# A hand-made order for VectorE, ScalarE and TensorE in the second part of a sparse graph-attention kernel

## The chip, the cores and the metric

The kernel runs on one core of a Trainium2 chip. The metric is the device time of one execution in microseconds. The kernel before took 1316.58 us (median of 9 runs, 1310.54 to 1321.33).

A core has five engines, each with its own queue of instructions that it takes in order: TensorE (PE; matrix multiplies, PEld is its loading of weights), VectorE (DVE), ScalarE (ACT), GpSimd (POOL) and SyncE (SP). An instruction that needs another engine's result waits on a semaphore, and what stands behind it on its engine waits with it. DMAs are issued from POOL and SP.

## The reference

3327 nodes with 1024 features in float32, and a symmetric 0/1 matrix `adj` of 3327 x 3327 with ones on the diagonal and few others:

```python
h = jnp.maximum(_layernorm(x, axis=-1), 0.0)
f = h @ Wf + bf
g = h @ Wg + bg
e = jax.nn.relu(f @ g.T)
scores = jnp.where(adj > 0, e, NEG)
attention = jax.nn.softmax(scores, axis=1)
x = x + attention @ (h @ W + bW)
```

Only the pairs that `adj` connects count. Some nodes have 37 neighbours, most 11 to 25.

## The kernel before, in words

The kernel works on the edges alone (`edge_path`; the dense path behind it runs only if a check finds a node with too many neighbours).

**First part (to about 250 us).** It reads `adj`, makes of each row a list of neighbours, normalises x into h (kept in HBM as `hd`), folds Wf and Wg into one matrix `A_sb` so that a node's score with a neighbour is a dot of q = h A (plus a bias) with the neighbour's h, and sorts the nodes by their number of neighbours. The change leaves this part alone.

**Second part.** The sorted nodes are taken in 26 tiles of 128. `CAPS` holds how many neighbours a tile can have; `ORDER` is the order of processing, and the text counts tiles in that order, 0 to 25. Tile 2 has 37 neighbours, tile 3 has 25, and so on down to 17 in tile 16, 13 in tiles 23 and 24 and 11 in tile 25. Tiles of more than 16 neighbours (2 to 16) are worked in two chunks: the first has 10 (19 in tile 2), the second the rest. The others have one chunk. A chunk is a *unit* of the main loop.

For each tile:

- GpSimd gathers the rows h of neighbour k, one per node, into one of 26 buffers G (`dot`, gather L983 through the helper at L356), and later gathers the tile's own x onto the result (`result`, L1097) and scatters the result out (`finish`, L1102). `fetch` (L894) brings the list and the own rows of a tile two tiles ahead.
- VectorE makes the *dots*: a row of G times q, added up, one score each (L986, followed by a short read of the accumulator). A dot reads all 1025 columns of q.
- `softmax`: VectorE takes relu and mask (L995) and the negated *maximum* of the chunk (L997; L999 joins it with the earlier chunk's). ScalarE makes the exponentials (L1002). For a second chunk it makes the factor `al` (L1005) and scales the running sum y by it (L1011); for a first chunk it scales row 0 by its weight, which becomes y (L1050). `l` and `rs` (L1006, L1009) are the total and its inverse.
- `combine`: the rows are added up with their weights. 11 per tile in tiles 3 to 23 (20 in tile 2, 5 to 7 in the others) are *sums* on VectorE (L1052), y += weight x G. The others, only in the tile's last chunk, are scaled on ScalarE (L1046) and added on TensorE, by transposing them into one PSUM accumulator (`sum_transposed`, L1026). `on_tensor` says how many.
- `project`: TensorE adds y itself to that accumulator, ScalarE copies it out (L1060), TensorE multiplies it with W (32 matmul records, L1068, 13.9 us), ScalarE scales the result (L1090).
- Meanwhile the q of the tile two ahead is made: `turned` transposes its own rows (L917), `taken` copies them (L924), `third` multiplies them with one third of `A_sb` (L936), `emptied` copies that third of q out on ScalarE (L946) and puts the bias into the freed PSUM bank (`filled`, L884). The last third stands after y's transposes in `project`, and its copy after the softmax of the next unit.
- `failed` (L1113), called once in tile 23, brings the check's flag together: a small matmul (L1120) and a cast on VectorE (L1121).

**What sets the order.** A planner orders the instructions of each engine in this part, by priority (roughly the program's order) and by what it reckons to be ready. `in_line` (L864) ties the marked instructions of TensorE and ScalarE into one chain in program order; the others, and all of VectorE and GpSimd, the planner places. With `AHEAD = 3`, the first three dots of the next unit are written behind a unit's softmax, the other dots of that unit at its beginning. In the program that results, VectorE alternates a tile's sums with dots of the next unit; behind the last maximum of a two-chunk tile comes a sum first, behind a first-chunk maximum come two to seven dots, and behind the maximum of a one-chunk tile one to three sums.

Of the kernel before, what the change touches and what calls it, by code (L numbers as in the profile page):

```python
# [33 lines left out]
AHEAD = 3  # L34
# [262 lines left out]
def edge_path(ctx: ExitStack, tc: tile.TileContext, x, adj, Wf, bf, Wg, bg, W, bW, out, flag):  # L297
# [563 lines left out]
    queue = {}  # L861

    @contextmanager
    def in_line():  # L864
        with ExitStack() as both:
            for ins in queue.values():
                both.enter_context(tc.issue_after(ins.ins))
            yield


# [15 lines left out]

    one = small.tile([P, 1], FP, name="one")
    tc.keep_in_program_order(nc.scalar.activation(one, ident[:, :1], AF.Exp))

    for at in range(2):  # L890
        filled(p_q, "ps_q", vb, QB, 6 + at, True)
        filled(p_o, "ps_o", bWb, CB, at, True)
# [15 lines left out]
    def turned(s):  # L908
        e = st[s]
        e["hT"] = hTpool.tile([P, KD, P], FP, name="hT")  # L910
        e["ps_t"] = []
        for g in range(0, KD, 4):
            ps = p_t.tile([P, 4, P], FP, name="ps_t")
            e["ps_t"].append(ps)
            with in_line():
                for k in range(4):
                    ins = nc.tensor.transpose(ps[:, k, :], e["hp"][:, (g + k) * P : (g + k + 1) * P], ident)  # L917
            queue["pe"] = ins

    def taken(s):  # L920
        e = st[s]
        for g, ps in enumerate(e["ps_t"]):
            with in_line():
                queue["act"] = nc.scalar.copy(e["hT"][:, 4 * g : 4 * g + 4, :], ps)  # L924

    def third(s, i):
# [7 lines left out]
        with in_line():  # L934
            for k in range(KD):
                ins = nc.tensor.matmul(  # L936
                    ps[:, :QB], e["hT"][:, k, :], A_sb[:, k, o : o + QB], start=False, stop=(k == KD - 1),
                    skip_group_check=True,
                )
        queue["pe"] = ins  # L940

    def emptied(s, i):
        e = st[s]
        at = 3 * ORDER.index(s) + i
        with in_line():
            ins = nc.scalar.copy(e["q"][:, i * QB : (i + 1) * QB], e["ps_q"][i][:, :QB])  # L946
            if at + 2 < 3 * NT:
                ins = filled(p_q, "ps_q", vb, QB, at + 2)
        queue["act"] = ins
# [29 lines left out]
    def dot(s, k, behind=None):  # L979
# [5 lines left out]
        with tc.issue_after(behind.ins) if behind else ExitStack():  # L985
            nc.vector.tensor_tensor_reduce(  # L986
                junk, g, e["q"][:, :D], 1.0, e["q"][:, D : D + 1], op0=ALU.mult, op1=ALU.add,
                accum_out=e["sc"][:, k : k + 1],
            )

    def softmax(s, k0, k1, last):
# [5 lines left out]
        nc.vector.tensor_reduce(nm, sc, AX.X, ALU.max, negate=True)  # L997
        if k0:
            nc.vector.tensor_tensor(nm, nm, e["nm"], op=ALU.min)  # L999
        l = small.tile([P, 1], FP, name="l")  # L1000
        with in_line():
            nc.scalar.activation(sc, sc, AF.Exp, bias=nm, accum_out=l)  # L1002
        if k0:
            al = small.tile([P, 1], FP, name="al")
            nc.scalar.activation(al, e["nm"], AF.Exp, bias=nm, scale=-1.0)  # L1005
            nc.vector.scalar_tensor_tensor(l, e["l"], al, l, op0=ALU.mult, op1=ALU.add)  # L1006
        if last:
            e["rs"] = small.tile([P, 1], FP, name="rs")
            nc.vector.reciprocal(e["rs"], l)  # L1009
        if k0:  # L1010
            queue["act"] = nc.scalar.activation(e["y"], e["y"], AF.Copy, scale=al)  # L1011
        e["nm"], e["l"] = nm, l
# [19 lines left out]
    def combine(s, k0, k1, last, ahead=None):  # L1032
        e = st[s]
        if not k0:
            e["y"] = G[s, 0]
# [3 lines left out]
        for k in range(k0, k1):  # L1039
            p = e["sc"][:, k : k + 1]  # L1040
            g = G[s, k]
            if k in pe:
                if k == pe[-1] and ahead is not None:
                    taken(ahead)
                with in_line() if k == pe[-1] else ExitStack():
                    queue["act"] = nc.scalar.activation(g, g, AF.Copy, scale=p)  # L1046
                queue["pe"] = sum_transposed(e, g, e["first"], False)
                e["first"] = False
            elif k == 0:
                queue["act"] = nc.scalar.activation(y, y, AF.Copy, scale=p)  # L1050
            else:
                e["summed"] = nc.vector.scalar_tensor_tensor(y, g, p, y, op0=ALU.mult, op1=ALU.add)  # L1052

    def project(s, then=None):
        e = st[s]
        yT = yTpool.tile([P, KD, P], FP, name="yT")
        with in_line():
            queue["pe"] = sum_transposed(e, e["y"], e["first"], True)
            for g in range(0, KD, 4):
                queue["act"] = nc.scalar.copy(yT[:, g : g + 4, :], e["yT"][:, g : g + 4, :])  # L1060
# [3 lines left out]
        for o in range(OH):  # L1064
            ps = banks.pop(("ps_o", OH * ORDER.index(s) + o))
            with in_line():
                for k in range(KD):
                    ins = nc.tensor.matmul(  # L1068
                        ps, yT[:, k, :], W_sb[:, k, o * CB : (o + 1) * CB], start=False, stop=(k == KD - 1),
                        skip_group_check=True,  # L1070
                    )
            e["o"].append(ps)
            queue["pe"] = ins
# [3 lines left out]
    def result(s):  # L1077
# [3 lines left out]
        for o in range(OH):  # L1081
# [7 lines left out]
            with in_line():  # L1089
                ins = nc.scalar.activation(to, ps, AF.Copy, scale=e["rs"])  # L1090
                if at < OH * NT:
                    ins = filled(p_o, "ps_o", bWb, CB, at, scale=st[ORDER[at // OH]]["l"])
            queue["act"] = ins
# [143 lines left out]
```

## Time and profile before

| | |
|---|---|
| median of 9 runs | 1316.58 us (1310.54 to 1321.33) |
| profiled execution, its own time | 1324.93 us |
| its span, first to last instruction | 1323.1 us |
| VectorE busy | 1157.7 us (87%) |
| TensorE busy | 1125.1 us (85%) |
| GpSimd, ScalarE busy | 892.6, 609.8 us |
| dots L986 | 468 of 1284 ns, 601.0 us |
| sums L1052 | 275 of 1286 ns, 353.5 us |
| mean granted TensorE clock | 0.941 |

The profile is of one execution. A line of a timeline gives the start, the duration, the engine, the line of the kernel, the operation, what it writes and reads, and in brackets how long its engine stood idle before it and what ended that. A line of waits gives the engine and operation that waited, what released it, the sum of the waits, their number and the longest. Durations of neighbours overlap a little, so the pace of an engine is read from start to start. Busy times of TensorE are modelled ends.

### The profile page before, as it was taken

What the parts mean: (1) busy time and instruction counts of PE and PEld (TensorE: products, weight loads), DVE (VectorE), ACT (ScalarE), POOL (GpSimd) and SP (SyncE); (2) the same over time, 40 slices, a digit from 0 to 9 for tenths busy, and PEclk for the clock granted to TensorE, in tenths of its full rate; (3) what the DMA queues carried; (4) which work ended last, traced back from release to release, by engine and by line L of the source; (5) the groups of instructions that cost most, each with busy time, mean ns of one, the idle gap of its engine ahead of it and who ended that gap; (6) DMA issues with size and microseconds to landing.
All of it is one profiled execution on the core that took longest, in us unless ns stands there. A gap on an engine that the chain in (4) does not pass through costs nothing.

```text
span 1323.1 us, 14316 instructions
## 1 busy us (share of the span) xinstructions
PE 1125.1 (85%) x4488; PEld 708.9 (54%) x4488; DVE 1157.7 (87%) x2205; ACT 609.8 (46%) x943; POOL 892.6 (67%) x678
## 2 busy tenths in 40 slices
PE   2799962967855999898899898999999899999995
PEld 2566631643525575566555555555655566555553
DVE  6899977575899889899999999999999999999980
ACT  5899976133306255345442554433344433333350
POOL 8999973384675777776766667676666666666611
PEclk9899985976977989999999999999999999999998
DMA  9999995786786998898888888888888688888821
GB/s 372 416 390 405 410 320 190 259 284 241 232 296 240 300 301 286 292 316 293 287 292 287 293 295 289 284 267 291 290 289 278 215 283 289 275 288 285 270 80 50
DMA packets 101802, 374.44 MB, mean 283 GB/s; under 512 B 14747, under 2 KB 18490, under 8 KB 98519
## 3 DMA queue, kind: packets, MB, share of 16 engines
q0 software_dynamic: 80624, 290.96, 66.1%
q1 hardware_dynamic: 21094, 82.49, 16.2%
q8 instruction: 37, 0.61, 0.2%
q14 instruction: 47, 0.39, 0.1%
HBM read 344.11 MB, written 29.30 MB: 282 GB/s over the span
## 4 chain that ended last, share of the span: by engine, by line
issue 30%; DVE 27%; PE 14%; DMA 12%; POOL 9%; ACT 7%; SPq 0%; POOLq 0%; another core or an unknown queue 0%; DVEq 0%; ACTq 0%
DVE G L1052 11%; POOL G L356 8%; DMA G<-hd,pi 5%; DVE junk L986 5%; DVE cand L482 5%; PE ps_o L1068 4%; PE yT_ps L1026 4%; PE ps_A L552 4%; ACT G L1046 3%; PE ps_q L936 2%; DMA r<-in_adj_dram 2%; DMA res<-in_x_dram,perm 1%; DVE sc L986 1%; DMA xt<-in_x_dram 1%; ACT G L1011 1%
## 5 line engine op out<-in xcount | busy, mean ns | idle before, releaser
L356 POOL DMA_INDIRECT G<-hd,pi x454 | 541.5, 1193 | 205.3 <-issue 100.6
L986 DVE CUSTOM_DVE_ANT_0 junk<-G,q 128x1024 bf16<-128x1024 f32 x468 | 601.0, 1284 | 39.5 <-DMA G<-hd,pi 18.1
L1052 DVE SCALAR_TENSOR_TENSOR G<-G,sc 128x1024 f32<-128x1024 f32 x275 | 353.5, 1286 | 39.9 <-ACT G L1011 22.6
L1068 PE MATMUL ps_o<-W_sb,yT 128*128 128x512 f32 x832 | 363.3, 594 | 6.3 <-ACT yT L1060 6.3
L936 PE MATMUL ps_q<-A_sb,hT 128*128 128x342 f32 x1152 | 347.7, 456 | 9.7 <-issue 9.4
L1026 PE MATMUL yT_ps<-ident,G 128*128 128x128 f32 x1544 | 211.0, 289 | 87.9 <-ACT G L1046 62.4
L936 PEld LDWEIGHTS ps_q<-A_sb,hT 128*128 128x128 f32 x1152 | 216.9, 192 | 119.8 <-issue 17.9
L1068 PEld LDWEIGHTS ps_o<-W_sb,yT 128*128 128x128 f32 x832 | 157.4, 189 | 200.6 <-issue 188.1
L1026 PEld LDWEIGHTS yT_ps<-ident,G 128*128 128x128 f32 x1544 | 182.0, 149 | 119.8 <-ACT G L1046 76.3
L419 POOL TENSOR_TENSOR r<-r,iotaj 128x1664 f32<-128x1664 f32 (+3 forms) x50 | 183.8, 3739 | 12.1 <-ACT r L412 12.1
L1046 ACT ACTIVATE G<-G,sc 128x1024 f32<-128x1024 f32 x167 | 182.4, 1142 | 0.0
L1002 ACT ACTIVATE sc<-sc,nm 128x10 f32<-128x10 f32 (+11 forms) x41 | 12.5, 304 | 343.3 <-DVE nm L999 251.7
L552 PE MATMUL ps_A<-WgT,WfT 128*128 128x342 f32 x432 | 131.5, 463 | 2.3 <-ACT WfT L547 2.3
L482 DVE MAX8 cand<-r 128x8 f32<-128x208 f32 (+2 forms) x416 | 119.1, 360 | 4.2 <-POOL r L419 3.3
L946 ACT COPY q<-ps_q 128x342 f32<-128x342 f32 x72 | 31.4, 437 | 166.4 <-PE ps_q L936 129.6
L552 PEld LDWEIGHTS ps_A<-WgT,WfT 128*128 128x128 f32 x432 | 82.2, 194 | 43.2 <-issue 3.0
L412 ACT ACTIVATE r<-r 128x3327 f32<-128x3327 int32 (+3 forms) x27 | 77.3, 2862 | 7.8 <-DMA r<-in_adj_dram 7.8
L356 POOL DMA_INDIRECT res<-in_x_dram,perm x25 | 43.2, 1727 | 51.3 <-ACT res L1090 43.4
L1102 POOL DMA_INDIRECT out_dram<-res,perm x25 | 30.7, 1226 | 69.2 <-DMA res<-in_x_dram,perm 67.7
L924 ACT COPY hT<-ps_t 128x512 f32<-128x512 f32 x48 | 25.4, 581 | 75.5 <-PE ps_t L917 75.5
L356 POOL DMA_INDIRECT pi<-pd,perm x26 | 29.6, 1139 | 34.6 <-DMA cd<-cand 17.9
L536 PE MATMUL ps_tr<-ident,A_sb 128*128 128x128 f32 x128 | 23.1, 343 | 26.5 <-DMA A_sb<-in_L_gnn_Wg_dram 23.3
(139 smaller groups left out, 718.7 us busy)
## 6 DMA issues: line engine op xcount, KB each, us to landing
r<-in_adj_dram SPq DMA_DIRECT2D x24, 1663.5 KB, 12.2
xt<-in_x_dram SPq DMA_DIRECT2D x25, 512.0 KB, 13.0
hd<-xt SPq DMA_DIRECT2D x25, 512.0 KB, 10.5
G<-hd,pi POOLq DMA_INDIRECT x454
A_sb<-in_L_gnn_Wg_dram SPq DMA_DIRECT2D x8, 512.0 KB, 17.3
A_sb<-in_L_gnn_Wf_dram SPq DMA_DIRECT2D x8, 512.0 KB, 11.8
W_sb<-in_L_gnn_W_dram POOLq DMA_DIRECT2D x1, 4096.0 KB
cd<-cand SPq DMA_DIRECT2D x25, 64.0 KB, 12.2
```

Source lines behind the costliest of these rows:

```text
L356: return nc.gpsimd.indirect_dma_start(out=to, out_offset=None, in_=table, in_offset=bass.IndirectOffsetOnAxis(ap=idx, axis=0), **kw,)
L412: nc.scalar.activation(r[:n, b:e], a[:n, b:e], AF.Sign, accum_out=to)
L419: eng.tensor_mul(r[:n, b:e], r[:n, b:e], iotaj[:n, b:e])
L482: nc.vector.max(cands[t][:n, s * 8 : s * 8 + 8], r[:n, s * SW : min(N, (s + 1) * SW)])
L552: nc.tensor.matmul(ps[:, :QB], WfTs[c][:, k, :], WgT[:, k, o : o + QB], start=(k == 0), stop=(k == KD - 1))
L936: ins = nc.tensor.matmul(ps[:, :QB], e["hT"][:, k, :], A_sb[:, k, o : o + QB], start=False, stop=(k == KD - 1), skip_group_check=True,)
L946: ins = nc.scalar.copy(e["q"][:, i * QB : (i + 1) * QB], e["ps_q"][i][:, :QB])
L986: nc.vector.tensor_tensor_reduce(junk, g, e["q"][:, :D], 1.0, e["q"][:, D : D + 1], op0=ALU.mult, op1=ALU.add, accum_out=e["sc"][:, k : k ...
L1026: ins = nc.tensor.matmul(e["yT"][:, c, :], g[:, c * P : (c + 1) * P], ident, is_transpose=True, start=(first and c % 4 == 0), stop=(last a ...
L1046: queue["act"] = nc.scalar.activation(g, g, AF.Copy, scale=p)
L1052: e["summed"] = nc.vector.scalar_tensor_tensor(y, g, p, y, op0=ALU.mult, op1=ALU.add)
L1068: ins = nc.tensor.matmul(ps, yT[:, k, :], W_sb[:, k, o * CB : (o + 1) * CB], start=False, stop=(k == KD - 1), skip_group_check=True,)
```

## The change

All instructions of the second part on VectorE, ScalarE and TensorE are put under `manual_schedule`: these three engines take them in the order in which the program writes them. The chain `in_line` and the tie of the last tile's dots to earlier sums go. GpSimd and SP stay with the planner.

The program's order is rewritten for it. `AHEAD` is 2: from the third unit on, two dots of the next unit are written behind each maximum, after the copy of q's last third. `combine` then takes a function `between`, which writes one more dot of the next unit after each sum. What is left of the unit's dots comes at its beginning. `softmax` writes `al`, the exponential and the scaling of y next to each other, and the totals move into a new function `totalled` behind the two dots. The matmul and cast of `failed` stay in their place in the program, behind the rest of tile 23 and ahead of tile 24; the loads of the flag move to the end.

```diff
-AHEAD = 3
+AHEAD = 2
...
-    def dot(s, k, behind=None):
+    def dot(s, k):
...
-    def softmax(s, k0, k1, last):
+    def softmax(s, k0, k1):
...
         nc.vector.tensor_reduce(nm, sc, AX.X, ALU.max, negate=True)
+        l = small.tile([P, 1], FP, name="l")
         if k0:
             nc.vector.tensor_tensor(nm, nm, e["nm"], op=ALU.min)
-        l = small.tile([P, 1], FP, name="l")
-        with in_line():
-            nc.scalar.activation(sc, sc, AF.Exp, bias=nm, accum_out=l)
+            e["al"] = small.tile([P, 1], FP, name="al")
+            nc.scalar.activation(e["al"], e["nm"], AF.Exp, bias=nm, scale=-1.0)
+        nc.scalar.activation(sc, sc, AF.Exp, bias=nm, accum_out=l)
         if k0:
-            al = small.tile([P, 1], FP, name="al")
-            nc.scalar.activation(al, e["nm"], AF.Exp, bias=nm, scale=-1.0)
-            nc.vector.scalar_tensor_tensor(l, e["l"], al, l, op0=ALU.mult, op1=ALU.add)
+            nc.scalar.activation(e["y"], e["y"], AF.Copy, scale=e["al"])
+        else:
+            e["y"] = G[s, 0]
+            nc.scalar.activation(e["y"], e["y"], AF.Copy, scale=e["sc"][:, :1])
+        e["nm"] = nm
+        e["ls"] = (e.get("l"), l)
+        e["l"] = l
+
+    def totalled(s, k0, last):
+        e = st[s]
+        if k0:
+            before, l = e["ls"]
+            nc.vector.scalar_tensor_tensor(l, before, e["al"], l, op0=ALU.mult, op1=ALU.add)
         if last:
             e["rs"] = small.tile([P, 1], FP, name="rs")
-            nc.vector.reciprocal(e["rs"], l)
-        if k0:
-            queue["act"] = nc.scalar.activation(e["y"], e["y"], AF.Copy, scale=al)
-        e["nm"], e["l"] = nm, l
+            nc.vector.reciprocal(e["rs"], e["l"])
...
             else:
-                e["summed"] = nc.vector.scalar_tensor_tensor(y, g, p, y, op0=ALU.mult, op1=ALU.add)
+                nc.vector.scalar_tensor_tensor(y, g, p, y, op0=ALU.mult, op1=ALU.add)
+                between()
...
+    with tc.manual_schedule(engines={
+        mybir.EngineType.Activation, mybir.EngineType.DVE, mybir.EngineType.PE
+    }):
...
+            dots(s, range(k0, k1))
...
+            softmax(s, k0, k1)
+            if late:
+                emptied(late.pop(), 2)
+            covered = AHEAD if i > 1 else 0
+            dots(s2, range(a, min(b, a + covered)))
+            totalled(s, k0, last)
...
+            coming = iter(range(a + covered, b) if i > 1 and s != ORDER[-2] else ())
+
+            def between(s2=s2, coming=coming):
+                for k in coming:
+                    dots(s2, [k])
+                    break
+
+            combine(s, k0, k1, last, ahead, between)
...
+                if not at or i + 1 == len(units) or units[i + 1][2] == CAPS[units[i + 1][0]]:
+                    rest()
+                    rest = None
+                if at + 2 == NT - 1:
+                    failed()
+        finish(done_with.pop())
+        bad = nc.values_load(flag[0:1, 0:1], min_val=0, max_val=1 << 20)
+        result(ORDER[-1])
+        finish(ORDER[-1])
```

In the resulting program VectorE has, for a two-chunk tile, "maximum, two dots, totals, sum, dot, sum, seven dots" and then, in the next tile's first chunk, "maximum, two dots, and nine times sum, dot". For a one-chunk tile it has "maximum, two dots, rs, eleven times sum, dot, and the dots that are left". Tiles 0 and 1 have their sums in a row and then their successor's dots.

## The prediction

> **What bounds the kernel now.** I read the page's busy times first, then the waits of VectorE in the second part, then the three engines in order of time around one maximum, and last the end of the execution.
>
> ```profile
> span 1323.1 us, 14316 instructions
> PE 1125.1 (85%) x4488; PEld 708.9 (54%) x4488; DVE 1157.7 (87%) x2205; ACT 609.8 (46%) x943; POOL 892.6 (67%) x678
> ```
>
> VectorE and TensorE are both nearly full. The second part runs from about 277 us; it holds 468 dots (L986) and 275 sums (L1052). On VectorE a dot or sum starts 1.20 us after its predecessor where the two kinds alternate, 1.33 us where a dot follows a dot. So 743 of them cost at least 892 us of about 1030. What VectorE still waits for in that part:
>
> ```profile
> DVE G L1052 <- ACT G L1011: 22.6, 15, 1.7
> DVE res L1084 <- PE ps_o L1068: 20.0, 2, 13.9
> DVE G L1052 <- ACT G L1050: 14.4, 10, 4.1
> DVE junk L986 <- ACT q L946: 14.1, 2, 13.8
> DVE l L1006 <- ACT al L1005: 6.5, 10, 0.7
> DVE rs L1009 <- ACT sc L1002: 2.9, 8, 0.5
> ```
>
> The first, third and last two lines are the waits after a maximum: 46.4 us in all, the most that covering them could win. The other two are one early wait and the end. Around one maximum (VectorE, then ScalarE):
>
> ```profile
> 727.64 0.15 DVE L999 TENSOR_TENSOR nm<-nm 128x1 f32<-128x1 f32 x1
> 728.44 0.22 DVE L1006 SCALAR_TENSOR_TENSOR l<-l,al 128x1 f32<-128x1 f32 x1 [0.65 <-ACT al L1005]
> 730.52 1.28 DVE L1052 SCALAR_TENSOR_TENSOR G<-G,sc 128x1024 f32<-128x1024 f32 x1 [1.66 <-ACT G L1011]
> ```
> ```profile
> 727.83 0.30 ACT L1002 ACTIVATE sc<-sc,nm 128x10 f32<-128x10 f32 x1 [18.23 <-DVE nm L999]
> 728.13 0.28 ACT L1005 ACTIVATE al<-nm 128x1 f32<-128x1 f32 x1
> 729.35 1.14 ACT L1011 ACTIVATE G<-G,al 128x1024 f32<-128x1024 f32 x1
> 730.39 0.42 ACT L946 COPY q<-ps_q 128x342 f32<-128x342 f32 x1
> 745.23 0.45 ACT L946 COPY q<-ps_q 128x342 f32<-128x342 f32 x1 [3.15 <-PE ps_q L936]
> 747.58 0.30 ACT L1002 ACTIVATE sc<-sc,nm 128x10 f32<-128x10 f32 x1 [1.42 <-DVE nm L997]
> ```
>
> See two things. The copy at 730.39 is the last third of the next tile's q: it starts 2.6 us after the maximum. And the copy at 745.23, first third of a later q, holds ScalarE back until TensorE delivers: 17.4 us after the maximum at 727.8; the next exponential stands behind it. VectorE arrives 1.4 us later than that, so nothing is lost. The end:
>
> ```profile
> 1239.02 0.19 PE L1120 MATMUL ps_t<-onesf,bad 128*1 128x1 f32 x2 [0.24 <-ACT hT L924]
> 1245.18 0.14 DVE L1121 CAST flag<-ps_t 1x1 int32<-1x1 f32 x1
> ```
>
> The check's matmul runs ahead of tile 23's y transposes here, and its cast fits between sums.
>
> **The change, part by part.** Tiles are counted in processing order. TensorE's matmuls keep their order, except the check's. ScalarE gets, after each maximum: (al), exponential, y scaling, copy of the last third, bias fill, then the row scalings. VectorE gets a fixed order. GpSimd's gathers keep their order by tile. In tiles 20 to 24 the gather-add of an earlier result now stands behind 1 to 4 of a tile's row gathers (3 to 5 before), and the fetch of a later tile's own rows (L904) behind some ten of them. Of 26 buffers a tile of 15 leaves 10 to run ahead, so I cost this at 0 and keep it as a rival. The finishing scatter still follows two gathers later. SP issues nothing that moves.
>
> *A. Two dots behind the maximum of a tile's last chunk, tiles 6 to 16.* They are dots of the next tile. A dot reads the whole q, so it waits for the copy of the last third, which in the new order follows exponential, al and y scaling: starts 0.04 + 0.20 + 0.10 + 0.18 + 1.04, copy 0.42, is 2.0 us. Today VectorE waits 0.65 + 1.66 = 2.3 us here in the tiles up to 11 and 1.2 us in tiles 12 to 16. So the wait is renamed, not covered. Dots following dots go from about 11 to 8 a tile: -3 x 0.13 = -0.4. Six cycles at -0.7, four at +0.4, plus 0.4 twice from B: about -2. A full walk of the same cycles (38.1 against 36.3 to 37.1 for 17 rows, 40.5 against 41.0 for 19) gives +3. I take 0; bounds -4 and +4.
>
> *B. The sums of the next tile's first chunk, tiles 3 to 6.* From last-chunk maximum to next maximum VectorE now has 2.0 wait, two dots 2.5, l and rs 0.35, sum-dot-sum 3.6, seven dots 9.2, maximum 0.35: 18.0 us; then two dots, so the first sum is due at 20.6. It also needs the exponential and y scaling behind ScalarE's copy of the first third, 2.5 us after that copy starts. The copy starts 28.8, 28.0, 23.6 and 19.5 us after the maxima at 406.19, 459.05, 509.23 and 556.42 (435.00, 487.00, 532.85, 575.95), because these tiles scale 16 to 10 rows on ScalarE at 1.05 us each. So the sum waits until 31.3, 30.4, 26.1, 22.0. Before, the planner filled this time with up to seven dots behind the maximum; now two. What is left after it: 9 sums and (rows - 12) dots, 27.7, 25.1, 23.7, 22.4 us for 25, 23, 22, 21 rows. Cycles 59.0, 55.5, 49.8, 44.5 against 52.9, 50.2, 47.2, 43.5 measured: +6.1, +5.3, +2.6, +1.0 = +15. Bounds: +8 if TensorE's clock is full here (it was not: below), +20.
>
> *C. Tiles of one chunk, 17 to 23.* The two dots again need the next q's last third, now produced late: last sum, y transposes 0.95 + 0.05, last third's matmuls 4.65, copy 0.45 + 0.05. That is 6.1 us, then two dots 2.5, rs 0.2, ten pairs 24.0, the eleventh sum 1.2: a cycle of 34.1 us from last sum to last sum, even where VectorE's own work for 13 rows is 31. Before, two sums stood behind the maximum and the dots waited for nothing. From 997.17 (tile 16) to the end of tile 23's projection at 1269.90 it was 272.7 us. Now: first maximum 26.3, plus 2.0, to the last sum 28.0 (56.2); tiles 18, 19, 20 each 34.3 by VectorE's own work; 21 to 23 each 34.1; projection 19.5: 281. +8. Bounds 0 (TensorE's own cycle, 32.2 us at 1107 to 1139, holds instead) and +12.
>
> *D. The check.* Its matmul now stands behind tile 23's projection on TensorE, and its cast stands ahead of tile 24's maximum in VectorE's queue. So VectorE stops until that projection ends (last sum + 19.5). Queued behind: all of tile 24 and 25. From the end of the projection: cast and maximum 0.75, wait 2.0, two dots 2.6, rs 0.2, six sums 7.2, nine dots 12.0, maximum 0.35, exponential and scaling 1.7, six sums 7.2: 34.0; y transposes and copy 1.5, projection 14.0: 49.5. Before: 1309.9 - 1269.9 = 40.0. +9.5; bounds +5 (TensorE idles less than I think) and +13.
>
> *E. The beginning.* Tiles 0 and 1 lose their interleaving: seven sums now run while VectorE waited 13.8 us for q; but row gathers behind the first gather-add land at 349 as before. Thirteen dots are done by then instead of twelve, and one less extra dot stands before the maximum: -2; bounds -6 and +3.
>
> Sum: 0 + 15 + 8 + 9.5 - 2 = +30.5. The profiled execution took 1324.93 us (span 1323.1), 0.6% over the median of 1316.58; its clock was low early, which touches B alone. So profiled 1355, and 1316.6 + 30.5 = 1347 for the median.
>
> *A rule that speaks against the change.* The row: TensorE waited 27.45 us before 407.90, and its granted clock was 0.61 in 380 to 400 and 0.70 in 400 to 420; after 5.30 us at 1054.22 it was 0.83 in that 10 us. The Trainium skill, TensorE: Matmul & The Clock Gate, section "Why this matters for your kernels", says that an idle gap over about 3 us drops the array to half its clock. By it B's longer cycles and D's idle would each cost one more slow window, 1 to 2 us, some +8 in all, 1355; I leave it out of the sum, as TensorE is rarely last in those places.
>
> **Rivals.** *The covers work (faster).* If the last third were copied before it is needed, the two dots would hide the waits: one mechanism, at each maximum. Price: up to 46.4 us, less D's 9.5 and TensorE's bound of 32.2 in C (0.6 x 7): near 1285. It decides if the copy ends within about 0.3 us of the maximum. Against: 730.39 shows it 2.6 us behind.
>
> *Only the end and C pay.* With full clock, B falls to +4: 1316.6 + 4 + 8 + 9.5 - 2 = about 1336. For: the low clock differs between executions.
>
> *Gathers become late.* If a result's gather-add blocks GpSimd while only one or two rows of the tile are fetched, VectorE waits for rows: 3 us (the longest such wait now) in 16 tiles on top: 1395. Against: only 8.8 us of row waits after 277.
>
> *It does nothing:* the waits merely change names everywhere and D hides behind the last matmuls: 1317.
>
> **How the numbers follow.** My forecast 0.62, only end and C 0.14, late gathers 0.12, nothing 0.05, covers work 0.07. The predicted time is 1347. Range 1326 to 1368: A to E at their low bounds together would be +3 and at their high bounds +52, unlikely all at once, so it holds about +9 to +51; it leaves out the covers, the nothing and most of the late gathers. 0.5% is about what a measurement of this kernel can tell from no change. Faster 0.07, same 0.05, slower 0.88.
>
> **What would show it.** A: dots behind last-chunk maxima waiting on ScalarE's q copy, about 2 us, 20 to 25 times. B: first sums of tiles 3 to 5 waiting 5 to 10 us for the y scaling. C: cycles of 34 us, TensorE with gaps of 1 to 2 us ahead of y transposes. D: the cast of the flag waiting 15 to 18 us for the check's matmul, and about 50 us from that projection to the last. I am wrong if the dots find q ready, if the cast does not wait, or if row gathers hold VectorE.

## The result, and the profile after

The changed kernel takes 1360.99 us (median of 10 runs, 1354.96 to 1364.09) against 1315.94 us (median of 31 runs, 1304.47 to 1325.31) of the kernel before: a ratio of 1.0338, 95% interval 1.0311 to 1.0365, which is slower by about 45 us. Predicted were 1347 us and a range of 1326 to 1368.

The profiled execution of the changed kernel took 1358.02 us (span 1356.1). That of the kernel before lay 9 us over the median of the 31 runs, this one lies 3 us under its own, so the two profiles differ by 33 us where the medians differ by 45. The first lines of the page of the changed kernel, and the waits of VectorE after 277 us:

```profile
span 1356.1 us, 14294 instructions
PE 1124.8 (83%) x4488; PEld 723.0 (53%) x4488; DVE 1160.0 (86%) x2205; ACT 612.2 (45%) x943; POOL 889.6 (66%) x678
```
```profile
DVE junk L961 <- ACT q L923: 35.4, 17, 3.3
DVE G L1030 <- ACT G L983: 33.0, 9, 13.2
DVE flag L1095 <- PE ps_t L1094: 18.2, 1, 18.2
DVE res L1060 <- PE ps_o L1045: 16.7, 2, 10.6
DVE junk L961 <- issue: 15.3, 5, 4.5
...
DVE junk L961 <- DMA G<-hd,pi: 1.0, 1, 1.0
```

The engines do the same work as before (VectorE 1160.0 against 1157.7 us, TensorE 1124.8 against 1125.1); only what VectorE waits for has changed. The first line is the dots (now L961) that wait for ScalarE's copy of q's last third; the second the first sums (now L1030) that wait for the scaling of y; the third the flag's cast. All three are waits that the prediction named. Three places on VectorE, then the same on ScalarE:

```profile
423.55 1.28 DVE L1030 SCALAR_TENSOR_TENSOR G<-G,sc 128x1024 f32<-128x1024 f32 x1 [13.18 <-ACT G L983]
...
729.08 0.16 DVE L975 TENSOR_TENSOR nm<-nm 128x1 f32<-128x1 f32 x1
731.26 1.28 DVE L961 CUSTOM_DVE_ANT_0 junk<-G,q 128x1024 bf16<-128x1024 f32 x1 [2.01 <-ACT q L923]
...
1290.10 0.15 DVE L1095 CAST flag<-ps_t 1x1 int32<-1x1 f32 x1 [18.19 <-PE ps_t L1094]
```
```profile
421.08 0.45 ACT L923 COPY q<-ps_q 128x342 f32<-128x342 f32 x1 [8.64 <-PE ps_q L915]
422.36 1.15 ACT L983 ACTIVATE G<-G,sc 128x1024 f32<-128x1024 f32 x1
...
729.28 0.29 ACT L977 ACTIVATE al<-nm 128x1 f32<-128x1 f32 x1 [18.20 <-DVE sc L970]
729.76 1.13 ACT L980 ACTIVATE G<-G,al 128x1024 f32<-128x1024 f32 x1
730.80 0.42 ACT L923 COPY q<-ps_q 128x342 f32<-128x342 f32 x1
```

At 729 the dot starts as the copy of 730.80 ends, 2.0 us after the maximum: term A's chain. At 421 ScalarE waits 8.64 us for TensorE's first third and only then comes to the scaling of tile 3's y, so VectorE stands for 13.18 us: term B's. The end, on TensorE:

```profile
1289.88 0.19 PE L1094 MATMUL ps_t<-onesf,bad 128*1 128x1 f32 x2
1293.57 8.15 PE L1009 MATMUL yT_ps<-ident,G 128*128 128x128 f32 x48 [3.51 <-ACT G L1026]
...
1304.81 14.00 PE L1045 MATMUL ps_o<-W_sb,yT 128*128 128x512 f32 x32 [0.68 <-ACT yT L1038]
...
1326.59 15.61 PE L1045 MATMUL ps_o<-W_sb,yT 128*128 128x512 f32 x32 [0.68 <-ACT yT L1038]
```

The check's matmul now stands behind the projection of tile 23, and the cast behind it.

Divided at the maxima that the prediction used, all profiles of this study give the following table, in us. E runs from the span's start to the last maximum of tile 2, B from there to that of tile 6, A to that of tile 16, C to the end of tile 23's projection, D to the start of the last result (the last projection's end). The kernel before has its own rows; the first pair are the profiles told of so far, and the experiments ran in three sets, each on a chip of its own.

| kernel | E | B | A | C | D |
|---|---|---|---|---|---|
| before, first profile | 406.2 | 193.7 | 397.3 | 272.7 | 40.0 |
| changed, first profile | 389.7 | 209.7 | 407.6 | 283.0 | 52.2 |
| set 1: before (e1) | 401.5 | 191.2 | 397.5 | 274.0 | 39.9 |
| check early (e2) | 391.6 | 209.1 | 407.6 | 287.9 | 39.9 |
| copy early (e3) | 397.3 | 205.5 | 390.8 | 282.2 | 50.9 |
| more cover (e4) | 392.1 | 192.6 | 405.5 | 284.0 | 50.8 |
| set 2: sums first (e5) | 389.1 | 198.5 | 406.4 | 272.9 | 56.1 |
| check split (e6) | 389.7 | 198.4 | 405.8 | 284.3 | 39.9 |
| no dots behind last chunks (e7) | 387.8 | 198.8 | 402.1 | 282.5 | 50.9 |
| all four (e8) | 391.5 | 180.7 | 385.6 | 270.9 | 39.9 |
| set 3: before (e9) | 403.1 | 187.7 | 397.5 | 274.4 | 39.9 |
| changed (e10) | 397.3 | 213.3 | 408.3 | 287.0 | 50.9 |
| sums first (e11) | 395.3 | 216.6 | 406.9 | 272.9 | 55.9 |
| check split (e12) | 397.4 | 213.1 | 410.2 | 287.6 | 39.9 |

The first pair: -16.5 (E), +16.0 (B), +10.3 (A), +10.3 (C), +12.2 (D), together +32.3 of the 33 by which the spans differ. The pair of set 3: -5.8, +25.6, +10.8, +12.6, +11.0, together +54.2 of 55.0. One thing is owed to the boundary between A and C: in the kernel before, the planner held the last two sums of tile 16's first chunk back behind its last maximum. So stretch A has 108 sums there and 110 in the changed kernel, and 2.4 us of A's difference belong to C.

```profile
997.01 0.16 DVE L999 TENSOR_TENSOR nm<-nm 128x1 f32<-128x1 f32 x1
997.13 1.28 DVE L1052 SCALAR_TENSOR_TENSOR G<-G,sc 128x1024 f32<-128x1024 f32 x1
...
998.46 1.28 DVE L1052 SCALAR_TENSOR_TENSOR G<-G,sc 128x1024 f32<-128x1024 f32 x1
```

### The profile page after: what moved, and what is told of

It reads as the page before. It is cut to its first block, busy times and chain, and to the rows that moved or that the text cites. A ratio compares the mean times of both kernels' runs of the same rounds, so it can differ in the third digit from the quotient of the medians.

```text
span 1356.1 us, 14294 instructions
## 1 busy us (share of the span) xinstructions
PE 1124.8 (83%) x4488; PEld 723.0 (53%) x4488; DVE 1160.0 (86%) x2205; ACT 612.2 (45%) x943; POOL 889.6 (66%) x678
## 4 chain that ended last, share of the span: by engine, by line
DVE 34%; issue 27%; PE 13%; DMA 12%; ACT 8%; POOL 6%; SPq 0%; POOLq 0%; DVEq 0%; ACTq 0%
DVE G L1030 17%; DVE junk L961 7%; POOL G L356 5%; DVE cand L482 4%; DMA G<-hd,pi 4%; ACT G L1026 3%; PE ps_o L1045 3%; PE yT_ps L1009 3%; PE ps_A L552 3%; DMA res<-in_x_dram,perm 2%; PE ps_q L915 2%; DVE sc L961 1%; DMA A_sb<-in_L_gnn_Wg_dram 1%; DMA G<-hd,perm 1%; DMA xt<-in_x_dram 1%
## 5 line engine op out<-in xcount | busy, mean ns | idle before, releaser
L356 POOL DMA_INDIRECT G<-hd,pi x454 | 525.1, 1157 | 224.2 <-issue 103.7
L961 DVE CUSTOM_DVE_ANT_0 junk<-G,q 128x1024 bf16<-128x1024 f32 x468 | 601.4, 1285 | 68.5 <-ACT q L923 35.4
L1030 DVE SCALAR_TENSOR_TENSOR G<-G,sc 128x1024 f32<-128x1024 f32 x275 | 353.5, 1285 | 34.2 <-ACT G L983 33.0
L915 PE MATMUL ps_q<-A_sb,hT 128*128 128x342 f32 x1152 | 341.6, 452 | 0.0
L1009 PE MATMUL yT_ps<-ident,G 128*128 128x128 f32 x1544 | 215.7, 301 | 108.8 <-ACT G L1026 73.4
L1009 PEld LDWEIGHTS yT_ps<-ident,G 128*128 128x128 f32 x1544 | 197.8, 157 | 130.7 <-ACT G L1026 82.0
L1026 ACT ACTIVATE G<-G,sc 128x1024 f32<-128x1024 f32 x167 | 179.1, 1140 | 0.0
L977 ACT ACTIVATE al<-nm 128x1 f32<-128x1 f32 x15 | 4.4, 294 | 301.8 <-DVE nm L975 171.9
L1076 POOL DMA_INDIRECT out_dram<-res,perm x25 | 35.5, 1420 | 72.3 <-DMA res<-in_x_dram,perm 70.8
L899 PE MATMUL ps_t<-ident,G 128*128 128x128 f32 x192 | 26.7, 285 | 26.6 <-DMA G<-hd,perm 26.6
```

The costliest lines, as they stand in the source:

```text
L356: return nc.gpsimd.indirect_dma_start(out=to, out_offset=None, in_=table, in_offset=bass.IndirectOffsetOnAxis(ap=idx, axis=0), **kw,)
L915: nc.tensor.matmul(ps[:, :QB], e["hT"][:, k, :], A_sb[:, k, o : o + QB], start=False, stop=(k == KD - 1), skip_group_check=True,)
L961: nc.vector.tensor_tensor_reduce(junk, g, e["q"][:, :D], 1.0, e["q"][:, D : D + 1], op0=ALU.mult, op1=ALU.add, accum_out=e["sc"][:, k : k ...
L1009: ins = nc.tensor.matmul(e["yT"][:, c, :], g[:, c * P : (c + 1) * P], ident, is_transpose=True, start=(first and c % 4 == 0), stop=(last a ...
L1076: ins = nc.gpsimd.indirect_dma_start(out=out[:, :], out_offset=bass.IndirectOffsetOnAxis(ap=perm[:, s : s + 1] if s < N // P else final, a ...
```

## The experiments

Line numbers in the text are those of the changed kernel. Each of e2 to e7 is the changed kernel with one edit.

**e1: the kernel before, a second profile.** It was to tell whether the long wait early in the first profile belongs to the order or was a disturbance.

> The kernel before once more, for a second profile of it. Theory (term E is small, and the first profile of before was disturbed early, with a 13.8 us wait for q in tile 1 at half clock): the last-chunk maximum of tile 2 comes near 390 us instead of 406.2, that wait shrinks to under 4 us, and the span is 8 to 16 us shorter, near 1310. Rival (the change itself made the beginning 16 us shorter): the maximum stands at 403 to 408 again, with the wait, and the span is 1320 or more.

It took 1319.27 us (span 1317.3), with the wait of 13.0 us and the last maximum of tile 2 at 401.5 us. Both figures lie a little below the rival's (403 to 408, 1320 or more) and far from the theory's (390, 1310), so the rival is the nearer. TensorE was late behind that wait; e9 shows it again.

**e2: the check early.**

```diff
                     third(ahead, 1)
+                if at + 2 == NT - 1:
+                    failed()
...
-                if at + 2 == NT - 1:
-                    failed()
```

> The changed kernel, with the check's matmul and cast moved back ahead of tile 23's y transposes and projection. Theory (term D: the cast holds VectorE until a projection has ended): the cast's wait falls from 18.2 us to under 3, the stretch from the end of tile 23's projection to the last projection from 52.2 to about 40 us, and the time by 10 to 13 us against the changed kernel (near 1349; 2.4 to 2.7% over before). Rival (the end is set by TensorE's last matmuls, and the cast's wait only moves to the result): within 3 us of the changed kernel.

1352.92 us, a ratio to before of 1.029 (1.0235 to 1.0345); the kernel before had 1313.58 us in this set, so the changed kernel at 1.0338 would stand at 1358. About 5 us came back, not 10 to 13. D is 39.9 us again, the cast waits 0.37 us; but C is 287.9, 5 us more than in the first profile of the changed kernel. TensorE, and the stretch behind its wait (columns: busy of TensorE, its weight loads, VectorE, ScalarE, GpSimd, with counts; granted clock; DMA share; GB/s):

```profile
1274.89 0.19 PE L1094 MATMUL ps_t<-onesf,bad 128*1 128x1 f32 x2 [3.26 <-DVE onesf L1092]
...
1275.93 6.46 PE L915 MATMUL ps_q<-A_sb,hT 128*128 128x342 f32 x16
1282.23 13.89 PE L1045 MATMUL ps_o<-W_sb,yT 128*128 128x512 f32 x32
```
```profile
1276.00:1283.00 7.00, 7.00 (x19) 4.22 (x19) 0.09 (x1) 3.09 (x7) 1.80 (x2) 0.76 0.78 283
```

VectorE's part of the check stood behind its last dots, so TensorE waited 3.26 us for it. VectorE's last sum had ended at 1273.43, and y's transposes, which need it, started at 1275.01; the last third then took 6.3 us (1275.93 to 1282.23) in place of 4.6, under a granted clock of 0.76. These two make 3.3 of the 5 us; the rest was there before the check (tile 23's last sum stands 1.7 us later, counted from tile 16's last maximum). The edit removed one wait and made another.

**e3: the copy of q's last third ahead of the exponential.**

```diff
             dots(s, range(k0, k1))
...
+            if late and k0:
+                emptied(late.pop(), 2)
             softmax(s, k0, k1)
```

> The changed kernel, with ScalarE's copy of the last third of q written ahead of the exponential behind the maximum of a second chunk (tiles of two chunks only). Theory (the two dots wait for that copy and for nothing else): the 2.02 us waits of the dots in tiles 2 to 16 go, and in tiles 6 to 16 the whole 2.0 us of a cycle is saved: 18 to 22 us less than the changed kernel (near 1341); the stalls of the first sums in tiles 3 to 6 stay or grow by 2 us each, as ScalarE's own place is what they wait for. Rival (the cycle is set by TensorE and ScalarE, the wait only names it): the same time appears as a longer wait at the next sum, and the kernel is within 5 us of the changed one.

1341.24 us, a ratio of 1.0179 (1.0117 to 1.0240): 17 us under the 1358 of e2's reckoning, 21 by the two ratios. Term A's stretch falls from 407.6 (e2, the same chip) to 390.8: 16.8 of the 20.2 us that ten waits of 2.02 make. The waits of VectorE after 277 us:

```profile
DVE G L1030 <- ACT G L983: 39.5, 10, 9.6
...
DVE junk L961 <- ACT q L923: 17.2, 6, 4.6
```

The six waits that are left on q are in tiles 17 to 24, which the edit leaves alone. The first sums wait longer (39.5 against 33.0 us): VectorE is earlier there and ScalarE is not. The kernel is also 7 us under before in stretch A (390.8 against 397.5): the change's form with the copy in the right place beats the planner's.

**e4: more dots behind first chunks.**

```diff
+COVER = {3: 12, 4: 10, 5: 4, 6: 3, 7: 3, 8: 3}
...
-            covered = AHEAD if i > 1 else 0
+            covered = COVER.get(at, AHEAD) if i > 1 and not (k0 or last) else AHEAD if i > 1 else 0
```

> The changed kernel, with more dots behind the maximum of a first chunk: 12, 10, 4, 3, 3, 3 in tiles 3 to 8 instead of 2. Theory (term B: the first sum waits for the y scaling behind ScalarE's copy of the first third, and only two dots cover it): the stalls of 13.2, 10.6, 2.6, 1.5, 1.1 and 1.0 us at the first sums fall to under 1 us each, cycles of tiles 3 and 4 go from 61.6 and 56.3 to about 52 and 50, where TensorE's own chain holds, and the time falls by 15 to 25 us against the changed kernel. Rival (ScalarE's copy moves with VectorE, so the covered work is waited for later): the stalls go but the cycles keep their length within 2 us, and the time is within 5 us.

1342.59 us, a ratio of 1.0210 (1.0156 to 1.0264), some 15 us under the same 1358. Stretch B falls from 209.1 (e2) to 192.6, the level of before (191.2); the cycles of tiles 3 and 4 become 54.1 and 47.0 (about 52 and 50 expected). The waits:

```profile
DVE junk L962 <- ACT q L924: 35.3, 15, 4.6
...
DVE junk L962 <- DMA G<-hd,pi: 11.5, 6, 4.2
...
DVE G L1031 <- issue: 3.3, 2, 2.3
DVE G L1031 <- ACT G L984: 3.2, 3, 1.2
```

The waits of the first sums fall from 33.0 to 3.2 us (6.5 with the two whose releaser the trace does not show). A part comes back as waits for gathered rows: the longest, 4.2 us, in tile 3, where twelve dots now ask for their rows early.

**e5 and e11: sums first in one-chunk tiles.** The edit ran in two sets, the second time beside the changed kernel.

```diff
-            covered = AHEAD if i > 1 else 0
+            covered = AHEAD if i > 1 and not (last and not k0) else 0
```

> The changed kernel, with no dots ahead of the first sum behind the maximum of a one-chunk tile (tiles 17 to 24); sums and dots then alternate. Theory (term C: the two dots need the next q's last third, which TensorE can deliver only 6.1 us after the last sum): the dots' waits of 2.0 to 4.6 us in tiles 17 to 23 go, a wait of 1.5 us for the y scaling stands in their place, the periods of 33 to 36 us become 32 to 33, and the time falls by 8 to 13 us. Rival (TensorE's own cycle sets the pace there): the periods stay within 0.5 us, the time within 4 us.

> Sums first in one-chunk tiles, now beside the changed kernel on one chip. From the earlier profiles (six periods of tiles 17 to 23 took 199.5 us against 204.5 to 204.9, but the end gave 0.5 back): 3 to 7 us less than the changed kernel. The first expectation (8 to 13) would need periods of 32 to 33 throughout.

In set 2 it took 1338.84 us (ratio 1.0331, 1.0304 to 1.0358). Beside the 1.0338 of the first result that is only 1 us less, where 8 to 13 were expected; the changed kernel had no run in that set. In set 3 it took 1362.26 against 1371.36 us of the changed kernel (ratio 1.0336, 1.0296 to 1.0377, against 1.0396): 9 us less, by medians and in the profiles, more than the 3 to 7 then expected. The dots' waits are gone, and stretch C falls from 287.0 to 272.9 (set 2: from 282.5 and 284.3 to 272.9), the level of before (272.7 to 274.4). The periods came to 34.0, 34.2, 34.1, 32.7, 32.9 and 31.5 us; 32 to 33 throughout, as I expected, was too low for the tiles of 15 neighbours. Of the 14 us in C, 5 are lost again in D, which grows from 50.9 to 55.9. VectorE at that place in e5:

```profile
1267.09 0.15 DVE L1095 CAST flag<-ps_t 1x1 int32<-1x1 f32 x1 [18.95 <-PE ps_t L1094]
1267.21 1.28 DVE L961 CUSTOM_DVE_ANT_0 junk<-G,q 128x1024 bf16<-128x1024 f32 x1
1268.54 1.28 DVE L961 CUSTOM_DVE_ANT_0 junk<-G,q 128x1024 bf16<-128x1024 f32 x1
```

The two dots that stood behind tile 23's maximum are now the last of tile 24's and stand behind the cast: 2.7 us on the path that sets the end. Most of the rest is the last projection, which takes 16.1 us here (1306.85 to 1323.0) against 14.0 in e7, behind an idle of TensorE of 2.67 us. So C and D are not independent costs: as long as the cast waits, a part of what is saved ahead of it is lost behind it.

**e6 and e12: the check in three places.** VectorE's reduction ahead of tile 23's sums, the matmul behind the second third, the cast behind the last sum.

```diff
-    def failed():
+    def flagged():
...
         nc.vector.memset(onesf, 1.0)
+        return worst, onesf
+
+    def failed(worst, onesf):
...
+            if at + 2 == NT - 1:
+                flags = flagged()
             combine(s, k0, k1, last, ahead, between)
...
                     third(ahead, 1)
+                if at + 2 == NT - 1:
+                    failed(*flags)
...
-                if at + 2 == NT - 1:
-                    failed()
```

> The changed kernel, with the check in three places: VectorE's reduction of it ahead of tile 23's sums, its matmul behind the second third of q, its cast behind tile 23's last sum. Theory (term D is all that the check costs; the earlier attempt lost half of it again because TensorE waited 3.3 us for the reduction, and its clock was 0.76 in the next 7 us): no wait of TensorE for the reduction, the projection of tile 23 ends within 20 us of its last sum (25 in the earlier attempt), the last projection 40 to 41 us later, and the time is 10 to 13 us under the changed kernel, 4 to 6 under the earlier attempt. Rival (half of D's cost is the two dots' wait at the end, not the check): within 3 us of the earlier attempt.

> The check in three places, now beside the changed kernel on one chip. The earlier profile's end (a 6.25 us wait of tile 24's dots for q's last third, in place of the flag's 18.2) would make 4 to 8 us less than the changed kernel; term D in full would make 10 to 13 less.

In set 2 it took 1337.07 us (ratio 1.0323, 1.0298 to 1.0347), 2 us less by the ratio of the first result where 10 to 13 were expected; in set 3 1355.76 us (1350.94 to 1363.95; ratio 1.0286, 1.0243 to 1.0330) beside 1371.36 of the changed kernel: 15.6 us by medians. The profiled execution was the slowest of its six; in the profiles the spans differ by 8.6 us. D is 39.9 in both sets, against 50.9: 11.0 us, term D in full. The 15.6 lie above the 10 to 13 expected; what the others of the six executions saved beyond D has no profile. TensorE has no wait for the reduction any more. VectorE in e6:

```profile
1258.10 0.14 DVE L1097 CAST flag<-ps_t 1x1 int32<-1x1 f32 x1
...
1258.50 0.17 DVE L972 TENSOR_REDUCE nm<-sc 128x1 f32<-128x13 f32 x1
1264.92 1.28 DVE L961 CUSTOM_DVE_ANT_0 junk<-G,q 128x1024 bf16<-128x1024 f32 x1 [6.25 <-ACT q L923]
```

The cast fits in with no wait. In its place the two dots of the next tile wait 6.25 us for q's last third: that is term C's chain at its last turn, no longer hidden behind the cast. D does not grow by it: from that projection on TensorE has work to the end, with two idle times of 0.68 us.

**e7: no dots behind the maximum of a second chunk.**

```diff
-            covered = AHEAD if i > 1 else 0
+            covered = AHEAD if i > 1 and not k0 else 0
```

> The changed kernel, with no dots ahead of the first sum behind the maximum of a second chunk (tiles 2 to 16). Theory (the two dots there only trade one wait for another, 2.0 us for q against 0.65 + 1.66 us for the scalings): dots' waits of 2.02 us go, waits of 2.3 us at the sums appear, and the time is within 4 us of the changed kernel. Rival (the order with two dots itself costs term A's 10.3 us in tiles 6 to 16, and without it they go as before): 8 to 12 us less.

1340.22 us, a ratio of 1.0344 (1.0321 to 1.0368), which is that of the changed kernel in the first result. Stretch A is 402.1 us against 406.4 and 405.8 in e5 and e6, whose code there is the changed kernel's: 4 us less. VectorE behind a last maximum:

```profile
586.45 0.16 DVE L975 TENSOR_TENSOR nm<-nm 128x1 f32<-128x1 f32 x1
587.26 0.22 DVE L992 SCALAR_TENSOR_TENSOR l<-l,al 128x1 f32<-128x1 f32 x1 [0.65 <-ACT sc L978]
...
588.30 1.28 DVE L1030 SCALAR_TENSOR_TENSOR G<-G,sc 128x1024 f32<-128x1024 f32 x1 [0.62 <-ACT G L980]
```

I had expected 2.3 us of waiting at the sums, the kernel before's. It is 1.27 us. The kernel before had a row scaling on ScalarE between `al` and the scaling of y, 1.04 us from start to start; in the new order none stands there:

```profile
728.31 1.13 ACT L1046 ACTIVATE G<-G,sc 128x1024 f32<-128x1024 f32 x1
```

So behind these maxima two dots wait 0.75 us longer than sums would, and cost 0.4 us a cycle more.

**e8: all four remedies.** The edits of e3, e5 and e6 together, and those of e4 with other numbers.

```diff
+COVER = {3: 9, 4: 9, 5: 6, 6: 7, 7: 4, 8: 4, 9: 3, 10: 3}
...
+            if late and k0:
+                emptied(late.pop(), 2)
             softmax(s, k0, k1)
...
-            covered = AHEAD if i > 1 else 0
+            covered = 0 if i < 2 or last and not k0 else AHEAD if k0 else COVER.get(at, AHEAD)
```

> All remedies together: the copy of q's last third ahead of the exponential behind second chunks; 9, 9, 6, 7, 4, 4, 3, 3 dots behind the first chunk's maximum in tiles 3 to 10; sums first in one-chunk tiles; the check in three places. Theory (A to D are separate costs, and what is left is VectorE's own work and TensorE's): the stalls go, tiles 3 to 6 take about 190 us, tiles 6 to 16 about 385, and the time falls by 45 to 60 us to 1300 to 1316, 0 to 1% under the kernel before. Rival (TensorE's chain takes up what VectorE no longer waits for): no better than 1325.

1283.28 us (1281.54 to 1283.82) against 1296.30 of the kernel before: a ratio of 0.9898, interval 0.9875 to 0.9921, which is faster than before by 1%, and 57 us under what the changed kernel's ratio would make. The waits of VectorE after 277 us:

```profile
DVE res L1061 <- PE ps_o L1046: 21.2, 2, 15.1
DVE G L1031 <- ACT G L984: 11.1, 11, 1.0
DVE rs L996 <- ACT sc L979: 5.1, 11, 0.5
DVE junk L962 <- DMA G<-hd,pi: 3.8, 1, 3.8
```

Of some 105 us of waits in the list of the changed kernel before its last two results, 20 are left. The stretch of tiles 2 to 6 takes 180.7 us (about 190 expected), that of 6 to 16 385.6: both under every profile of the kernel before, which has none on this chip.

**e9 and e10: both kernels on one chip.**

> The kernel before, beside the changed one on one chip, for a look at the beginning and at TensorE's waits for nothing visible (37 and 34 after 240 us in its first two profiles, none in the four profiles of the second set of experiments). Theory (those waits made the early wait of 13 us for q, and term E is small without them): if this profile has none of them, no 13 us wait stands in tile 1, tile 2's last maximum comes within 4 us of the changed kernel's, and the span is near 1295; if it has them, the wait stands there again and the span is 1308 to 1320. Rival (the wait belongs to the order of before): it stands there in both cases.

> The changed kernel beside the kernel before, on one chip. Theory: a ratio of 1.030 to 1.037 on any chip, and the terms A, C and D as in its first profile; without TensorE's waits for nothing visible the stalls of the first sums in tiles 3 and 4 are 7.7 and 4.6 us, not 13.2 and 10.6, and term E is -4 to 0. Rival (the change costs more where TensorE is slower to get its instructions): a ratio under 1.028 without those waits.

The kernel before took 1317.46 us in its profiled execution (median of the set 1319.79), the changed kernel 1371.36 (1365.17 to 1373.82), a ratio of 1.0396 (1.0355 to 1.0437). In e9 the wait for q stood there again (7.63 us), together with TensorE's waits for nothing visible. TensorE in e9, in e10, and in e7 at the place of e10:

```profile
305.48 0.45 PE L936 MATMUL ps_q<-A_sb,hT 128*128 128x342 f32 x1 [0.74 <-issue]
306.88 0.45 PE L936 MATMUL ps_q<-A_sb,hT 128*128 128x342 f32 x1 [0.96 <-issue]
```
```profile
312.50 15.89 PE L1045 MATMUL ps_o<-W_sb,yT 128*128 128x512 f32 x32 [11.82 <-issue]
...
414.26 0.54 PE L1009 MATMUL yT_ps<-ident,G 128*128 128x128 f32 x3 [0.45 <-issue]
415.69 0.27 PE L1009 MATMUL yT_ps<-ident,G 128*128 128x128 f32 x1 [0.89 <-issue]
```
```profile
407.94 1.09 PE L1009 MATMUL yT_ps<-ident,G 128*128 128x128 f32 x8 [0.52 <-ACT G L1026]
408.88 9.37 PE L915 MATMUL ps_q<-A_sb,hT 128*128 128x342 f32 x32
```

The standstill before 312.50 is no such wait, though the profile names nothing that ended it. ScalarE in e10:

```profile
311.86 1.07 ACT L1038 COPY yT<-yT_ps 128x512 f32<-128x512 f32 x2 [10.42 <-remote]
```

The projection reads this copy and starts as its first half ends. By the trace TensorE had written what it copies by 296.1; in e7 the same copy starts at 294.81. So it is ScalarE that stood idle here, for something that the profile does not name ("remote"), and TensorE waited for it; so it was in e2, e3, e11 and e12.

Eight transposes take 1.1 us in e7; in e10 they come one to three at a time, with 0.4 to 1.0 us of nothing between. In the chain of tile 3 this delays the first third of q, and with it the scaling of y that VectorE's first sum waits for: 12.8 us in e10, 8.2 us in e7. Adding up all rows of TensorE after 240 us for which the profile names nothing gives 34 of them and 25.6 us in e9, 22 and 28.4 us in e10 (11.8 of them the standstill), and none in the four profiles of set 2; some may be ordinary waits whose end the profile missed. The ratio of 1.0396 lies above the 1.030 to 1.037 expected for any chip. The rival (under 1.028 without those waits) fell as well: e7, without them, stands at 1.0344 although its edit saves 4 us in A. The changed kernel's stretch B is 15 us shorter in set 2 (198.4 to 198.8 against 213.3, where these rows add up to 10.0 us), but the kernel before is faster on that chip too. How far the chip matters for the ratio, not for the time, is open. Nor is there a profile of the kernel before without them, so whether its early wait would vanish is open too.

## Why the prediction was right, and where it was not

The forecast, slower by about 30 us by way of waits that change places, held in its direction and its places; 1361 lies 14 us over the 1347. That the first pair's +32.3 is so near to the sum of +30.5 is luck: A is 10 us over its term, E 14.5 under. By the steps:

- **A: wrong, 0 predicted, +10.3 and +10.8 measured, above the upper bound of +4.** The dots wait 2.02 us exactly as worked out. The step that failed is "dots following dots go from about 11 to 8 a tile: -3 x 0.13 = -0.4", which made a gain of 4 us over the ten cycles. Summed from the timelines, dots followed dots 90 times before and 80 times after, one fewer per tile and not three; and sums follow sums 15 times (1.32 us from start to start) where none did before. So dots and sums cost about 2 us more rather than 4 less, apart from the 2.4 us of the boundary. The short instructions around the maxima cost 2.3 us more (13.1 against 10.8), which I had not counted. The idle time grows by 3.6 us (22.2 against 18.6): by 1.6 at the last maxima, where I had 1.4, and by 2.1 at the first sums of two first chunks, which I had put at 0.4 each. The full walk, which gave +3 and which I did not take, was nearer: cycles of 38.1 and 40.5 us, measured 38.7 and 41.0. What the order costs, e3 and e7 show: the copy in front gives 16.8 us, and two dots cost 4 more than none.
- **B: right: +15 predicted, +16.0 measured in the first pair.** The cycles were forecast at 59.0, 55.5, 49.8 and 44.5 and measured at 61.6, 56.3, 47.2 and 44.7. e4 removes it (-16.5). In set 3 the same term is +25.6, above the upper bound of +20: of the 9.6 us more, 6.0 are the kernel before, which is shorter there (187.7 against 193.7), and 3.6 the changed kernel. TensorE's slow rows lie in this chain, but how much of the term they make was not shown; I had put "full clock or not" there as the unknown.
- **C: right: +8 predicted, +10.3 measured (12.6 in set 3).** The six periods from last sum to last sum were forecast at 205.2 us together and measured at 207.2. Of the 2.0 us missing 1.6 are in the first (35.9 against 34.3): behind an idle of TensorE of 4.51 us the y transposes took 1.5 us in place of 0.95 and the last third 5.7 (to 1070.49) in place of 4.65, at a granted clock of 0.81 in 1062 to 1071. e11 takes the whole term away.

```profile
1063.28 1.69 PE L1009 MATMUL yT_ps<-ident,G 128*128 128x128 f32 x8 [4.51 <-DVE G L1030]
1064.76 5.89 PE L915 MATMUL ps_q<-A_sb,hT 128*128 128x342 f32 x16
```

- **D: right in kind, too small: +9.5 predicted, +12.2 measured (11.0 in set 3).** The cast waited 18.19 us (15 to 18 forecast). Of the 2.7 us missing 1.6 are the last projection: 15.65 us (1326.59 to 1342.24) against 14.0, behind an idle of 2.51 us. e6 and e12 bring D to 39.9.
- **E: wrong in size: -2 predicted, -16.5 in the first pair, -5.8 in set 3.** The step that failed is "row gathers behind the first gather-add land at 349 as before". GpSimd's first gather-add, before and after:

```profile
341.12 1.69 POOL L356 DMA_INDIRECT res<-in_x_dram,perm  x1 [7.35 <-ACT res L1090]
```
```profile
322.75 2.02 POOL L356 DMA_INDIRECT res<-in_x_dram,perm  x1 [5.11 <-ACT res L1065]
```

The gather-add waits for tile 0's result, which waits for its projection, and this came 18 us earlier, as TensorE was not held up at 295 to 316 us. In set 3, where both kernels are late at this place (e10 by ScalarE's copy), the difference is 5.8. The changed order has 387.8 to 397.4 in E over its profiles, the kernel before 401.5 to 406.2, and no profile of it without the hold-up. So most of the -16.5 is probably a difference between executions, which would also be why the profiles differ by less than the medians.

**The rule of the Trainium skill.** TensorE: Matmul & The Clock Gate, section "Why this matters for your kernels", would have made an estimated 1355, nearer to the result than the sum, but not for its reason: the slow stretches behind idle times of 4.51 and 2.51 us cost 1.6 us in C and 1.6 in D, and the 10 us of A are none of it. Its effect is there in rows: behind the 3.51 us of idle that end at 1293.57 the granted clock was 0.77 in 1290 to 1305, behind the 4.51 us in C 0.81, and in e2 0.76 in the 7 us behind an idle of 3.26. But it is not a matter of 3 us alone: in e6 the clock was 0.73 in 1258.0 to 1264.2, and the last third took 6.3 us, behind idle times of 1.77 and 1.82 us only; in e12, behind idle times of 1.77 and 1.80, it was 1.00 and the third took 4.6.

**The rivals.** *Covers work* fell, but named the right lever: the copy ahead of the exponential (e3, e8) is its condition. *Only the end and C pay* fell: B cost 16.0 us in the first pair and A 10. *Late gathers* fell: 1.0 us of waits for rows in the changed kernel's first profile and 12.1 in its second (e10), against 8.8 to 11.6 before, where the rival needed 48 more. *It does nothing* fell: the cast does not hide (D).

## What to carry to other kernels

Work put behind a wait covers it only if it does not itself need something that is queued behind the same instruction: two dots that read all of q waited for a copy that stood behind the exponential and the scaling, and cost 0.4 us a turn more than no dots. When an order is written out by hand, each engine's queue has to be walked at each wait: the one copy moved up by four instructions was worth 17 us, the number of dots behind six maxima 16, the place of a check of a few tiny instructions 11. And when a wait goes, look at what stood hidden behind it: e2's edit lost 3 of its 12 us again, and that of e5 and e11 5 of its 14, to what stood next in the same queues.

## What the runs showed of the hardware

- In all profiles of sets 1 and 3 and of the first pair TensorE had stretches in which it ran one to three matmuls at a time with 0.2 to 1.5 us of idle between for which the profile names no cause; the four of set 2 have none, and the kernel before took 1296.30 us there, against 1313.58 and 1319.79 in the other sets. They come at the same places in one program (about 410, 470 and 525 us in the changed kernel). What TensorE waits for there was not shown; the load of its instructions is a guess that no run here tested.
- In e2, e3, e10, e11 and e12 ScalarE started its copy of tile 0's yT (at 304.8 to 312.9 us) 7 to 16 us after TensorE had written what it reads, by the trace, and TensorE's projection waited for it (3.2 to 11.8 us). The cause was not shown.
- The granted clock fell to 0.73 behind two idle times of 1.8 us in one execution and not in another of the same program (e6, e12).
